# Layer 2's begin: six 1x1 products go ahead of the 3x3 taps, and three of the first sample's twelve shifted quarters are copied by VectorE

## The chip, the cores and the metric

The kernel runs on one core of a Trainium2 chip. The metric is the device time of one execution in microseconds (us), and the figure compared is the median of several runs. The profile is one further execution; all times inside it count from the first instruction.

Of the core's engines, TensorE multiplies matrices (PE in the profile, PEld for its weight loads), VectorE (DVE) and ScalarE (ACT) work element by element, GpSimd (POOL) does so too and issues DMAs through software, and SyncE (SP) issues DMAs.

## The reference

Four layers run over an activation of 8 samples, 128 channels and 56 x 56 pixels. Every layer is `x = x + conv(group_norm(x))` with 32 groups. Layer 0 is an attention over windows, layer 1 a recurrence over the pixels, layer 3 a residual block of two 3x3 convolutions. The change lies in layer 2:

```python
m3 = (j - i) % p == 0                       # p = 4
w3m = w3 * m3[:, :, None, None]
out = conv_general_dilated(x, w3m, window_strides=(1, 1), padding=((1, 1), (1, 1)))
w1m = w1 * (~m3)
out = out + einsum('oi,bihw->bohw', w1m, x)
out = out + b.sum(axis=1)[None, :, None, None]
```

So a 3x3 convolution joins only channels whose numbers are equal modulo 4, which makes four separate groups of 32 channels, and a 1x1 product joins the channels of different groups.

## The kernel before

All eight samples stay in SBUF in one tile, `X`. Layer 2 goes through them sample by sample, and through each sample in 7 blocks of 8 image rows (448 pixels). A block is numbered `n` = 7 x sample + block, 56 in all.

**The taps (`within`, line 1343).** `g3` holds, for each of the four groups (`r`), three copies of that group's 32 normalized channels, shifted by k = 0, 1 and 2 columns and stacked on 96 partitions. Twelve of these shifted quarters fill `g3` for one sample. A tap is then one product of 96 x 32 weights for one row offset `dy` and one group; a block has 3 x 4 of them. In the profile every fp32 product is two instructions, so a block's taps are 24.

**The 1x1 product (`between`, line 1351).** One product of 128 x 128 weights reads the block's rows from the normalized, zero-bordered sample (`pads`) and adds to the same PSUM bank. `add` (line 1358) then adds bank and bias to `X`. The banks come from a pool of four.

**Getting a sample ready.** `Norm` makes the group norm: `stats` (line 1281, VectorE, one instruction a block and an aggregate), a small product that averages over the groups (`mean_mm`, line 1287), four small VectorE steps (`mean_end`), a second small product (`var_mm`, line 1299), the square root on ScalarE (`root`, line 1303), the reciprocal (line 1307) and `normal` (line 1314), which writes the normalized rows to `pads`. `normal` goes by five chunks of rows, cut at 0, 10, 18, 34, 50 and 58 of the 58 padded rows. `spread` (lines 1331 and 1333) fills `g3` for one chunk: the three quarters with r equal to k are ScalarE copies, the nine others are DMAs, for every sample six from GpSimd's queue and three from SyncE's.

**What sets the order.** TensorE, ScalarE, VectorE and GpSimd take their instructions in the order in which the program lists them (`manual_schedule`); SyncE's order comes from a planner. Before the loop over blocks the program lists sample 0's norm, 26 warm-up products on TensorE (line 897), the first statistics of sample 1, sample 0's square root, five times `normal` and `spread`, the masking of the 1x1 weights (`w1` times `m1`, line 1562), the bias sum (line 1563) and sample 1's other statistics. `w1`, `m1`, the bias matrix and the batch-norm parameters are loaded by SyncE just before (lines 1251 to 1262), once memory of layer 1 is free. In the loop, `mean_mm` of the next sample follows the taps of a sample's block 1 and `var_mm` those of block 2; 1x1 products and additions come in pairs, after every odd `n`; after block 3 the next sample is normalized, and its `spread` is listed at blocks 3, 4 and 6. `g3` is single, so a chunk of it is overwritten only when the taps that read it are done.

Of the kernel before, what the change touches and what calls it, by code (L numbers as in the profile page):

```python
# [20 lines left out]
P = 128  # L21
# [25 lines left out]
def conv_stack_kernel(ctx: ExitStack, tc: tile.TileContext, a: dict, out: bass.AP):  # L47
# [1158 lines left out]
    def convolutions(held=None):  # L1206

        with ExitStack() as l2:
# [32 lines left out]


            p2 = ExitStack()
            pool2 = p2.enter_context(tc.tile_pool(name="pool2", bufs=1))
            ps_c = p2.enter_context(tc.tile_pool(name="ps_c", bufs=4, space=PSUM))
            pads = [pad3, padded(pool2, "pad2", [P, PW, PW])]
# [73 lines left out]
            def spread(b, c):  # L1320
# [4 lines left out]
                for r in range(4):  # L1325
                    for k in range(3):
                        n = hi - lo - k
                        dst = g3[k * CL : (k + 1) * CL, r, lo : lo + n]
                        src = flat[r * CL : (r + 1) * CL, lo + k : lo + k + n]
                        if r == k:  # L1330
                            nc.scalar.copy(dst, src)
                        else:
                            (nc.sync, nc.gpsimd)[(r + k) % 2].dma_start(dst, src)

            pcs = {}

            def within(n):

                i = n % NBLK
                pcs[n] = ps_c.tile([P, WS, HW], F32, name=f"pc2_{n}", tag="pc")  # L1340
                for dy in range(3):
                    for r in range(4):
                        nc.tensor.matmul(  # L1343
                            pcs[n][r * CL : (r + 1) * CL], w3[:, dy, r, :],
                            rows3[:, r, i * WS + dy : i * WS + dy + WS, :HW], start=(dy == 0), stop=False,
                        )

            def between(n):

                b, i = divmod(n, NBLK)  # L1350
                nc.tensor.matmul(  # L1351
                    pcs[n], w1, pads[b % 2][:, 1 + i * WS : 1 + (i + 1) * WS, 1 : 1 + HW], start=False, stop=True
                )
# [193 lines left out]
            with ExitStack() as order:  # L1547
# [8 lines left out]
                warm(26, ps_g, "pg")  # L1556
                norms[1].stats(0)
                norms[0].root()
                for c in range(5):
                    norms[0].normal([c])  # L1560
                    spread(0, c)
                nc.vector.tensor_mul(w1, w1, m1)
                nc.vector.tensor_reduce(bsum, bmat, AX.X, ALU.add)
                for i in range(1, NBLK):
                    norms[1].stats(i)
                for n in range(B * NBLK):
# [11 lines left out]
                    if n % 2:  # L1578
                        between(n - 1)
                        between(n)  # L1580
                        add(n - 1)
# [450 lines left out]
```

## Time and profile before

| what | us |
|---|---|
| median of 3 runs (3253.56 to 3254.7) | 3254.4 |
| the profiled execution | 3253.89 |
| its span, first to last instruction | 3251.9 |
| layer 2's first tap, after the span's start | 2653.48 |
| TensorE busy in the span | 3178.3 |

The granted TensorE clock is 0.994 of full speed over the span. The profile page gives busy shares, groups of instructions by line and the chain of waits; the trace behind it gives the same for any stretch, and a timeline. A timeline's line has the start, the duration, the engine, the line of the kernel, what is written from what, and how many instructions were merged. A bracket at its end names how long the engine was idle before and whom it waited for. `g` stands for `g3`, `pad` for `pads`, `pc` for the banks, `st_l` and `mv_l` for the statistics, `pm_l` for the mean.

### The profile page before, as it was taken

How to read it: one execution, taken by the hardware profiler on the slowest of the kernel's cores; microseconds unless marked ns; L12 is line 12 of the kernel's file. 1: busy time of each engine (PE TensorE's matmuls, PEld its weight loads, DVE VectorE, ACT ScalarE, POOL GpSimd, SP SyncE). 2: the span in 40 equal slices, each digit the busy share in tenths (PEclk: the TensorE clock that was granted, in tenths of full speed). 3: DMA queues.
4: the chain of work that ended last, by engine and by line, in shares of the span. 5: the costliest groups of instructions: out<-in, count | busy, mean ns of one | idle time of the engine just before them, and what ended most of it. 6: DMA issues, size and time to landing. Idle time of an engine off the chain costs nothing.

```text
span 3251.9 us, 104559 instructions
## 1 busy us (share of the span) xinstructions
PE 3178.3 (98%) x40784; PEld 2679.8 (82%) x40784; DVE 2270.8 (70%) x5756; ACT 1270.3 (39%) x2425; POOL 1475.3 (45%) x4147
## 2 busy tenths in 40 slices
PE   8999999999999989999999999999999999999998
PEld 5767677676766679999999999999999973399998
DVE  5888888888887866666555555555532347799998
ACT  4555555555555532221111111111111244556564
POOL 4888888888777843333222222222200036522221
PEclk8999999999999999999999999999999999999999
DMA  5555555555455421110000000000022236500001
GB/s 156 135 143 131 143 137 138 142 135 143 120 137 145 121 63 49 49 49 29 1 1 1 1 1 1 1 1 1 8 58 61 59 104 166 144 16 36 31 36 46
DMA packets 188167, 239.09 MB, mean 74 GB/s; under 512 B 42848, under 2 KB 137568, under 8 KB 187664
## 3 DMA queue, kind: packets, MB, share of 16 engines
q0 software_dynamic: 40896, 123.47, 14.0%
q1 hardware_dynamic: 130256, 101.95, 10.9%
q10 hardware_dynamic: 16512, 6.90, 0.9%
q8 instruction: 324, 5.31, 0.7%
q14 instruction: 179, 1.47, 0.2%
HBM read 133.64 MB, written 67.56 MB: 62 GB/s over the span
## 4 chain that ended last, share of the span: by engine, by line
PE 83%; DVE 10%; issue 2%; POOL 2%; ACT 1%; DMA 1%; ACTq 0%; POOLq 0%; DVEq 0%; SPq 0%
PE ps L1086 27%; PE q L1051 9%; PE po L1116 5%; PE s L539 5%; PE po L605 5%; PE pc L1343 4%; PE t L581 4%; PE plep L420 4%; PE pc3a L1663 3%; PE pc3b L1663 3%; PE pi L1021 3%; DVE nmax L546 2%; PE t L571 2%; PE pc L1351 1%; PE py L446 1%
## 5 line engine op out<-in xcount | busy, mean ns | idle before, releaser
L1086 PE MATMUL ps<-hs,w_gates 128*128 128x136 f32 x7680 | 928.8, 279 | 0.0
L1086 PEld LDWEIGHTS ps<-hs,w_gates 128*128 128x128 f32 x7680 | 911.6, 190 | 4.5
L1100 ACT ACTIVATE hs<-v 128x272 f32<-128x272 f32 x538 | 212.3, 404 | 1167.3 <-DVE v L1098 1167.3
L546 DVE TENSOR_REDUCE nmax<-s 128x2 f32<-128x512 f32 x784 | 486.3, 684 | 169.3 <-PE s L539 167.6
L591 ACT ACTIVATE e<-t 128x512 f32<-128x512 f32 x784 | 429.5, 596 | 339.8 <-PE t L581 261.8
L1098 DVE TENSOR_TENSOR v<-ps,g 128x272 f32<-128x272 f32 x538 | 216.3, 411 | 494.6 <-PE ps L1086 407.3
L1039 POOL TENSOR_TENSOR d<-inp 128x136 f32<-128x136 f32 x186 | 87.8, 472 | 789.1 <-DVE inp L1027 789.1
L498 POOL COPY ks<-kT 128x64 f32 x1568 | 297.2, 235 | 120.6 <-PE t L581 69.0
L605 PE MATMUL po<-e,ring 128*32 128x64 f32 x12544 | 244.9, 230 | 6.1 <-DVE nmax L546 5.5
L605 PEld LDWEIGHTS po<-e,ring 128*32 128x32 f32 x12544 | 217.9, 149 | 31.0 <-DVE nmax L546 7.9
L581 PE MATMUL t<-qm,ks 32*128 32x128 f32 x6272 | 237.3, 273 | 1.3 <-issue 1.3
L539 PE MATMUL s<-ks,qm 32*128 32x256 f32 x3136 | 233.9, 403 | 4.4 <-ACT vp L342 2.3
L581 PEld LDWEIGHTS t<-qm,ks 32*128 32x128 f32 x6272 | 220.1, 187 | 3.3 <-issue 2.2
L1663 PE MATMUL pc3a<-va,u_w1c_t 128*128 128x196 f32 x1152 | 198.3, 330 | 7.6 <-POOL va L1517 5.8
L1116 PE MATMUL po<-hs,xw 128*128 128x272 f32 x744 | 204.1, 397 | 0.2
L1663 PEld LDWEIGHTS pc3a<-va,u_w1c_t 128*128 128x128 f32 x1152 | 190.4, 189 | 13.6 <-POOL va L1517 11.0
L1663 PE MATMUL pc3b<-vb,u_w2c_t 128*128 128x196 f32 x1152 | 195.8, 328 | 0.0
L1663 PEld LDWEIGHTS pc3b<-vb,u_w2c_t 128*128 128x128 f32 x1152 | 191.7, 189 | 0.0
L539 PEld LDWEIGHTS s<-ks,qm 32*128 32x128 f32 x3136 | 146.6, 185 | 34.4 <-issue 4.7
L1051 PE MATMUL q<-d,mixed 128*128 128x136 f32 x1116 | 160.2, 279 | 0.5 <-DVE g L1065 0.3
L500 POOL TENSOR_TENSOR qm<-q,hmask 128x128 f32<-128x128 f32 x392 | 154.0, 393 | 0.0
L1116 PEld LDWEIGHTS po<-hs,xw 128*128 128x128 f32 x744 | 132.0, 190 | 22.1 <-ACT hs L1100 0.6
(317 smaller groups left out, 5372.3 us busy)
## 6 DMA issues: line engine op xcount, KB each, us to landing
ring<-vpix SPq DMA_DIRECT2D x1176, 32.0 KB
v<-vimg POOLq DMA_DIRECT2D x56, 290.0 KB, 4.0
v<-vimg POOLq DMA_DIRECT2D x56, 289.5 KB, 4.8
v<-vimg POOLq DMA_DIRECT2D x56, 289.0 KB, 5.7
kept<-g SPq DMA_DIRECT2D x56, 272.0 KB, 2.4
g<-kept SPq DMA_DIRECT2D x56, 272.0 KB, 2.6
xkeep<-X POOLq DMA_DIRECT2D x56, 224.0 KB, 2.7
vimg<-vrow POOLq DMA_DIRECT2D x54, 232.0 KB, 2.7
```

Source lines behind the costliest of these rows:

```text
L498: nc.gpsimd.tensor_copy(kw[:, t : t + 1, :], ks[b][:, bass.ds(at, 1), :])
L539: nc.tensor.matmul(s_["s"][g][:, o, :], w["qm"][h].rearrange("p h x -> p (h x)"), w["kw"][h], start=True, stop=True,)
L546: nc.vector.tensor_reduce(s_["nmax"][:, :, g], s_["s"][g], AX.X, ALU.max, negate=True)
L581: nc.tensor.matmul(s_["t"][g][:, o, c], w["kw"][h, c * P : (c + 1) * P], w["qm"][h].rearrange("p h x -> p (h x)"), start=False, stop=(o == ...
L591: nc.scalar.activation(s_["e"][g], s_["t"][g], AF.Exp)
L605: mm = nc.tensor.matmul(po[g * CL : (g + 1) * CL, h, o], flat[:, at : at + 8 * CL - 7 : 8], s_["e"][g][:, o, c, h * WPX : (h + 1) * WPX], ...
L1051: nc.tensor.matmul(q[n // 3][:, n % 3], w, x, start=True, stop=True)
L1086: nc.tensor.matmul(ps[f][:, i], whh[:, k, m * P : (m + 1) * P], prev[k // 2][:, (s - 1) % 2, k % 2].rearrange("p c b -> p (c b)"), start=( ...
L1098: nc.vector.tensor_tensor(v[:, i : i + n], ps[f][:, i : i + n], x, ALU.add)
L1100: nc.scalar.activation(to, x, AF.Tanh)
L1116: nc.tensor.matmul(po, wout[:, k, :], hs[k // 2][:, :, k % 2], start=(k == 0), stop=(k == KH - 1))
L1663: nc.tensor.matmul(bank[:, half].rearrange("p (y x) -> p y x", x=H4), u[:, dy, k, :], v[:, k, i * RB + dy : i * RB + dy + RB, :], start=(d ...
```

## The change

- The pool of banks has six instead of four.
- The 1x1 products of the first six blocks are issued before the loop, behind the normalization of sample 0, and open their banks; the taps of these blocks then add to the bank and close it. Later blocks are as before.
- For sample 0 alone, the three quarters of group r = 3 are VectorE copies. Of the six DMAs left per chunk, three are on SyncE's queue and three on GpSimd's (before: three and six).
- The masking of `w1` stands ahead of sample 0's square root and reciprocal, not behind the normalization.
- `spread` of a chunk is listed one `normal` later, and the first statistics of sample 1 join the six others behind all this.

```diff
+            AHEAD = 6
-            ps_c = p2.enter_context(tc.tile_pool(name="ps_c", bufs=4, space=PSUM))
+            ps_c = p2.enter_context(tc.tile_pool(name="ps_c", bufs=AHEAD, space=PSUM))
...
                         if r == k:
                             nc.scalar.copy(dst, src)
+                        elif b == 0 and r == 3:
+                            nc.vector.tensor_copy(dst, src)
                         else:
-                            (nc.sync, nc.gpsimd)[(r + k) % 2].dma_start(dst, src)
+                            even = (r - k) % 3 == 2 if b == 0 else (r + k) % 2 == 0
+                            (nc.sync if even else nc.gpsimd).dma_start(dst, src)
...
             def within(n):
                 i = n % NBLK
-                pcs[n] = ps_c.tile([P, WS, HW], F32, name=f"pc2_{n}", tag="pc")
+                if n >= AHEAD:
+                    pcs[n] = ps_c.tile([P, WS, HW], F32, name=f"pc2_{n}", tag="pc")
                 for dy in range(3):
                     for r in range(4):
                         nc.tensor.matmul(
                             pcs[n][r * CL : (r + 1) * CL], w3[:, dy, r, :],
-                            rows3[:, r, i * WS + dy : i * WS + dy + WS, :HW], start=(dy == 0), stop=False,
+                            rows3[:, r, i * WS + dy : i * WS + dy + WS, :HW],
+                            start=(dy == 0 and n >= AHEAD), stop=(dy == 2 and n < AHEAD),
+                            skip_group_check=True,
                         )
             def between(n):
                 b, i = divmod(n, NBLK)
+                if n < AHEAD:
+                    pcs[n] = ps_c.tile([P, WS, HW], F32, name=f"pc2_{n}", tag="pc")
                 nc.tensor.matmul(
-                    pcs[n], w1, pads[b % 2][:, 1 + i * WS : 1 + (i + 1) * WS, 1 : 1 + HW], start=False, stop=True
+                    pcs[n], w1, pads[b % 2][:, 1 + i * WS : 1 + (i + 1) * WS, 1 : 1 + HW],
+                    start=(n < AHEAD), stop=(n >= AHEAD), skip_group_check=True,
                 )
...
                 warm(26, ps_g, "pg")
-                norms[1].stats(0)
+                nc.vector.tensor_mul(w1, w1, m1)
                 norms[0].root()
-                for c in range(5):
-                    norms[0].normal([c])
-                    spread(0, c)
-                nc.vector.tensor_mul(w1, w1, m1)
+                for c in range(6):
+                    if c < 5:
+                        norms[0].normal([c])
+                    if c > 0:
+                        spread(0, c - 1)
+                for n in range(AHEAD):
+                    between(n)
                 nc.vector.tensor_reduce(bsum, bmat, AX.X, ALU.add)
-                for i in range(1, NBLK):
+                for i in range(NBLK):
                     norms[1].stats(i)
...
                     if n % 2:
-                        between(n - 1)
-                        between(n)
+                        if n >= AHEAD:
+                            between(n - 1)
+                            between(n)
                         add(n - 1)
                         add(n)
```

## The prediction

> **What bounds the kernel now.** I read the profile page's busy shares first, then the windows of layer 2, its chain of waits, the timeline of its first 20 us, and last the groups kept apart by shape, for prices.
>
> ```profile
> span 3251.9 us, 104559 instructions
> ...
> PE 3178.3 (98%) x40784; PEld 2679.8 (82%) x40784; DVE 2270.8 (70%) x5756; ACT 1270.3 (39%) x2425; POOL 1475.3 (45%) x4147
> ```
>
> TensorE is busy in 98% of the span, so a change in order can only win where it is idle. The windows of layer 2's first two samples (columns: stretch, its length, then busy time and count of each engine, clock, DMA share, GB/s):
>
> ```profile
> 2653.40:2675.60 22.20, 22.09 (x172) 9.69 (x176) 10.57 (x19) 9.62 (x15) 13.06 (x28) 1.00 0.74 195
> 2675.60:2698.00 22.40, 22.40 (x190) 7.96 (x186) 12.69 (x26) 13.14 (x18) 16.44 (x34) 1.00 0.73 195
> ```
>
> From its first tap to the layer's end TensorE does not pause, and VectorE (third pair) has about half of its time free. The chain of waits over the begin (start, us, what):
>
> ```profile
> 2650.96 2.52 DMA g<-pad
> 2653.48 5.17 PE pc L1343 x48
> 2658.64 0.31 PE pm_l L1287 x2
> 2658.95 1.62 PE pc L1351 x4
> ...
> 2666.61 1.71 PE pc L1351 x4
> 2668.32 4.65 PE pc L1343 x48
> ```
>
> Two blocks' taps take 4.65 us undisturbed, 5.17 at the start; two blocks' 1x1 products take 1.71. The timeline around it:
>
> ```profile
> 2644.75 7.68 PE L897 MATMUL warm<-c_gavg 128*128 128x128 f32 x52
> ...
> 2645.42 3.12 DVE L1314 TENSOR_SCALAR pad<-X,gm_l,r_l 128x504 f32<-128x504 f32 x5
> ...
> 2645.98 0.43 SPq L1255 DMA_DIRECT2D m<-in_m_dram  x1
> ...
> 2648.46 0.28 DVE L1562 TENSOR_TENSOR w<-w,m 128x128 f32<-128x128 f32 x1
> ...
> 2648.85 3.25 DVE L1281 BATCH_NORM_STATS2 st_l<-X 128x6 f32<-128x448 f32 x6
> ...
> 2653.48 5.17 PE L1343 MATMUL pc<-g,w 96*32 96x448 f32 x48 [1.05 <-DMA g<-pad]
> ...
> 2658.99 0.16 DVE L1291 COPY gm_l<-pm_l 128x1 f32<-128x1 f32 x1 [6.03 <-PE pm_l L1287]
> ```
>
> Two things are to be seen. The warm-up products end at 2652.43, so only 1.05 us of idle TensorE lies ahead of the taps. And VectorE has sample 1's statistics ready six microseconds before TensorE asks for their mean (L1287, after the second block): that slack is what the change spends.
>
> **Ceiling of the gain.** The TensorE work is the same before and after. What idleness can go is 1.05 us ahead of the taps, 5.17 - 4.65 = 0.52 in the first two blocks, and 0.03 in the third: 1.60 us.
>
> **Products ahead.** Six products are 3 x 1.71 = 5.13 us. They follow the warm-up: 2652.43 to 2657.56, then two blocks of taps (4.65) to 2662.21. Their inputs are there: the last of them starts at 2656.7, and the fourth piece of the normalization it reads ends near 2655 by the sum below. The flags and the two more banks cost nothing: before, TensorE never waits for VectorE to free a bank in this layer, so a deeper ring hides nothing more; were a bank late, block 6 would wait for the addition of block 0, which ends some 9 us ahead of it.
>
> **The mask product moved up on VectorE.** It now stands ahead of the reciprocal and waits for m1, which SP issues at 2645.98. The old wait instruction for it, at 2648.1, lasted 0.05 us, so the data was there; the shortest landing of any spread transfer is 1.8, so not before 2647.8. I take 2648.1, the row of that very transfer. Queued behind it: reciprocal, five normalizations, fifteen copies, seven statistics; waiting on those: ScalarE's copies, both DMA queues, TensorE. Start to start, product to next 0.19 and reciprocal to normalization 0.20: the first normalization starts at 2648.49 instead of 2645.42, 3.07 later. SP loses nothing, since parameter loads hold its queue until 2649.38; POOL's first issue goes from 2646.51 to about 2649.6.
>
> **Three quarters by VectorE.** Fifteen copies, 10,077 elements in all (three times 3,364 columns, less the shifts). Rows:
>
> ```profile
> L1314 DVE TENSOR_SCALAR pad<-X,gm_l,r_l 128x504 f32<-128x504 f32 x1 | 0.8, 799 | 0.0
> ...
> L1176 DVE COPY first<-hs 128x256 f32<-128x256 f32 x2 | 0.6, 288 | 0.3 <-ACT hs L1100 0.3
> ...
> L1386 DVE TENSOR_SCALAR u_w1c_t<-u_w1c_t 128x768 f32<-128x768 f32 x1 | 0.5, 547 | 0.0
> ...
> L1375 DVE COPY u_w1c_t<-t_w1c_t 128x384 f32<-128x384 f32 x1 | 0.4, 406 | 0.0
> ```
>
> 256 and 768 elements at 288 and 547 ns give 0.51 ns an element and 0.16 us fixed. The 504 row (nine rows, an unbroken run into a padded one) is much slower, while the even 896 of the same line takes 738. Five of the fifteen have odd length (k = 1), so they might be slow as the 504 is; but the 384 copy is of three rows, odd too and alike on both sides as our copies are, and is fast. I take the fast price: 15 x 0.15 + 10.08 x 0.52 = 7.5, and 0.03 more each, the step between dependent VectorE instructions in the timeline: 7.95 us. The other end, every copy at one element per 1.04 ns (what the plain 128x136 copy out of PSUM, 295 ns, leaves after the fixed part): 12.75 + 0.45 = 13.2. The low end is 6.5, should they overlap by some 0.07 as the normalizations do (0.74 us long, 0.66 apart).
>
> **VectorE's sum.** 2648.49, five normalizations 3.04 (2645.42 to 2648.46), copies 7.95, the bias sum 0.20, seven statistics and their aggregate 3.28 + 0.53 + 0.34 = 4.15 (the first of them was free while the variance was awaited; now it is in line): 2663.83, and 0.10 to reach TensorE. TensorE wanted the mean at 2662.21: **a new stall of 1.72 us**. Sums of the ends: 2662.4 or less with the low price (no stall worth naming), 2669.2 with the high one (7.0).
>
> **Six quarters by DMA.** POOL issues 15 instead of 30 and SP 15 as before. At 0.50 each POOL is done near 2658 instead of 2664.65. Chunk 1, needed at 2659.9 by block 1, is issued by SP at 2653.2 at the latest, as before, and the landing seen on SP there is 5.3: 2658.5. ScalarE's fifteen copies (11.6) end at 2661, each chunk ahead of its block. Both are hidden by the 5.13 us of products that now go first; a transfer later by more than 1.4 us would show one for one, first by eating the stall at L1287 and then beyond it.
>
> **A rule against it.** POOL's first two issues, beside the normalizations, read 0.88 and 0.65 us instead of 0.50:
>
> ```profile
> 2646.51 0.88 POOL L1333 DMA_DIRECT2D g<-pad  x1 [0.73 <-DVE pad L1314]
> 2647.39 0.65 POOL L1333 DMA_DIRECT2D g<-pad  x1
> 2648.04 0.50 POOL L1333 DMA_DIRECT2D g<-pad  x1
> ```
>
> At 0.88 for all fifteen, chunk 1's last is issued by 2654.9 and lands 3.6 later at 2658.5: still hidden. The Trainium skill, "SBUF — State Buffer", section "Who interferes with whom", has a VectorE copy in its two-port mode shut GpSimd out of the shared port for the whole instruction; the page's example is a GpSimd DMA going from about 620 to 3100 ns. An estimate by that factor of five is 2.5 us an issue, chunk 2 then landing near 2675 where 2664 is needed, some 11 us lost. The rows go against a factor that large.
>
> **The next sample's begin.** What is late next: block 7, sample 1's first. Its normalization starts when block 3 is added, and its first chunk's last POOL issue stands at 2673.59 and lands 2.7 later: 2676.29, that is 7.97 us after block 3 ends (2668.32). Before, block 7 starts 8.68 us after it; without the products of blocks 4 and 5 it could start after 6.98, so it now waits for the DMA at 7.97. The change gets back 0.71 here and not 1.71.
>
> **Sum.** Mean product ends 2663.93 + 0.31, two blocks 2 x 2.39 and the variance 0.31: block 3 ends at 2669.33. Block 7 starts at 2669.33 + 7.97 = 2677.30 against 2677.00 before (2674.67 + 2.33): **+0.3 us**. From there the order is the old one and TensorE has no slack to give it back. The profiled execution took 3253.89 (span 3251.9); the median, 3254.4, is 0.5 above. With it: 3254.7.
>
> **The rivals.**
> 1. The cover holds fully: copies overlap, m1 is early, the DMA for block 7 too. All 1.60 us are won: 3252.8. For it: the low ends above; against it: VectorE must save 1.7 us.
> 2. The copies run at the slow price: 5.25 us more in the same stall, +5.5: 3259.9. For it: the 504 row; against it: the three copies and scalings above.
> 3. Slower: VectorE's copies wait at the port for POOL's issues, one each, 15 x 0.50 = 7.5 us more ahead of L1287: +7.8, 3262.2. It decides from 6.2 us, or 0.41 a copy. For it: the two stretched issues show that the engines meet; against it: the normalizations beside them kept their time (742 ns for 896 elements, 738 over all nine).
>
> A measurement of this kernel can tell about 0.2%, 6.5 us, from no change: 3247.9 to 3260.9.
>
> **How the numbers follow.** Forecast (between rival 1 and +3 us) 0.62, rival 1 0.12, rival 2 0.13, rival 3 0.11; 0.02 for a gain past the ceiling. Same is 0.62 + 0.12 + 0.13 = 0.87, slower 0.11, faster 0.02. The range takes in the forecast and rivals 1 and 2: 3252.6 to 3260.5.
>
> **What would show it.** After: six products right behind the warm-up, taps near 2657.6; the first normalization near 2648.5; copies of 0.39 to 0.63 us; a wait of TensorE for L1287's statistics of 1 to 2 us; block 7 waiting on a transfer by about 1 us. Wrong if m1 is loaded in another place of SP's order, if copies take over 0.8 us, if POOL's issues pass 1.5 us, or if TensorE stalls in a later sample.

## The result and the profile after

The changed kernel takes 3261.68 us (median of 19 runs, 3257.26 to 3265.68) where the kernel before takes 3255.74 (19 runs, 3253.0 to 3260.56). The ratio is 1.0017, with a 95% interval of 1.0011 to 1.0023: 5.9 us more. That is less than the 0.2% that the prediction took as the least that can be told from no change, but the interval separates it from zero, and it lies 1.2 us above the range that was forecast (3252.6 to 3260.5). The prediction was wrong: it had +0.3 us. Two executions of all those below, one of e10_half_filled and the profiled one of b_again, took 5334 and 4541 us at a granted clock of 0.56 and 0.65, and no comparison uses them.

The page of the changed kernel, first the span and then the busy time of each engine:

```profile
span 3260.6 us, 104551 instructions
...
PE 3184.0 (98%) x40784; PEld 2680.5 (82%) x40784; DVE 2280.4 (70%) x5771; ACT 1271.0 (39%) x2425; POOL 1474.0 (45%) x4132
```

TensorE has as many instructions as before and is busy 5.7 us longer (3184.0 against 3178.3). So a part of the loss is no idleness at all: the same products took longer. VectorE has 15 instructions more and GpSimd 15 fewer, which are the copies and the DMAs they replace.

The timeline around layer 2's begin (start, duration, engine, line, what is written from what, count, in brackets the idle time before):

```profile
2645.24 6.05 PE L897 MATMUL warm<-c_gavg 128*128 128x128 f32 x52
2646.49 0.43 SPq L1256 DMA_DIRECT2D m<-in_m_dram  x1
2648.66 0.29 DVE L1567 TENSOR_TENSOR w<-w,m 128x128 f32<-128x128 f32 x1 [3.77 <-DMA m<-in_m_dram]
2649.06 1.22 DVE L1315 TENSOR_SCALAR pad<-X,gm_l,r_l 128x504 f32<-128x504 f32 x2
2650.31 1.39 DVE L1334 COPY g<-pad 32x580 f32<-32x580 f32 x3
2651.13 3.19 PE L1360 MATMUL pc<-pad,w 128*128 128x448 f32 x8
2654.55 1.93 DVE L1334 COPY g<-pad 32x928 f32<-32x928 f32 x3
2654.58 1.78 PE L1360 MATMUL pc<-pad,w 128*128 128x448 f32 x4 [0.26 <-DVE pad L1315]
2656.28 4.72 PE L1348 MATMUL pc<-g,w 96*32 96x448 f32 x48
2657.22 3.16 DVE L1334 COPY g<-pad 32x928 f32<-32x928 f32 x6
2660.59 3.77 DVE L1282 BATCH_NORM_STATS2 st_l<-X 128x6 f32<-128x448 f32 x7
2664.40 0.34 DVE L1284 BATCH_NORM_AGGREGATE mv_l<-st_l 128x2 f32<-128x42 f32 x1
2664.80 0.59 PE L1288 MATMUL pm_l<-mv_l,c_gavg 128*128 128x1 f32 x2 [3.80 <-DVE mv_l L1284]
2665.32 4.71 PE L1348 MATMUL pc<-g,w 96*32 96x448 f32 x24
2670.47 12.85 PE L1348 MATMUL pc<-g,w 96*32 96x448 f32 x102
```

The mask waits 3.77 us for its load, and everything on VectorE stands behind it: normalization, copies, statistics. TensorE, done with the first two blocks at 2661.0, waits 3.80 us for sample 1's statistics. What the forecast has nothing of comes after that: block 2's 24 taps take 4.71 us, and the next 102 take 12.85, where runs of the same taps below take 2.46 and 10.6. The windows over the same stretch (stretch, length, then busy time and count of PE, PEld, DVE, ACT and POOL, then the granted clock, DMA share and GB/s) say why:

```profile
2656.00:2661.00 5.00, 5.00 (x49) 1.45 (x48) 4.87 (x10) 4.88 (x6) 2.86 (x5) 1.00 0.93 238
2661.00:2665.00 4.00, 0.20 (x2) 0.20 (x2) 3.96 (x9) 0.59 (x2) 0.00 (x0) 0.98 0.76 228
2665.00:2670.00 5.00, 5.00 (x27) 1.34 (x27) 3.12 (x9) 0.00 (x0) 0.00 (x0) 0.50 0.02 6
2670.00:2673.00 3.00, 3.00 (x22) 1.24 (x22) 0.68 (x1) 0.26 (x1) 0.00 (x0) 0.50 0.00 0
2673.00:2680.00 7.00, 7.00 (x68) 2.10 (x64) 4.72 (x7) 2.52 (x4) 1.65 (x4) 0.85 0.15 38
```

The granted clock is 0.50 from 2665 to 2673 and averages 0.85 to 2680: half speed for about 10 us, some 5 us of work lost, right behind a wait of 3.8 us. In the kernel before, the clock dips on the warm-up products, whose result nobody waits for (0.57 over 2644.7 to 2648.5), and stays at 1.00 from the first tap on.

The Trainium skill, "TensorE: Matmul & The Clock Gate", sections "What's actually happening" and "Why this matters for your kernels", states that an idle window of about 3.4 us halves the clock, that this window runs on its own and is not started by the kernel, and asks for no gaps above some 3 us. The 3.80 us here agree. The runs below agree with a window that runs on its own (the clock changes only in steps of 3.41 us, as shown under e0_third), but not with 3 us as a safe bound: the clock fell behind waits of 2.74 and of 1.55 us as well, and did not behind one of 2.70.

**A sum by stages.** Layer 1, whose code is the same, ends up to 5.6 us earlier or later from profile to profile, so stages are counted from the first small product of sample 0's mean (2642.69 on the trace before, 2643.17 after). Before, layer 2 lasts 201.94 us from there (201.22 in a second profile of the same kernel); after, 210.25: 8.3 more.

- Up to sample 1's mean product: 21.63 after, 15.88 before, but with six 1x1 products done, which last 5.13 by the forecast's row. Lost: 0.62.
- From there to the pair of products of blocks 6 and 7: 21.15 after; 20.68 before with those 5.13 in it, so 15.55. Lost: 5.60, almost all of it the clock.
- From there to layer 3: 167.47 after, 165.38 before. Lost: 2.1, in samples whose code did not change.

### The profile page after: what moved, and what is told of

Its sections match the earlier page's. It is cut to its first block, busy times and chain, and to the rows that moved or that the text cites. A ratio compares the mean times of both kernels' runs of the same rounds, so it can differ in the third digit from the quotient of the medians.

```text
span 3260.6 us, 104551 instructions
## 1 busy us (share of the span) xinstructions
PE 3184.0 (98%) x40784; PEld 2680.5 (82%) x40784; DVE 2280.4 (70%) x5771; ACT 1271.0 (39%) x2425; POOL 1474.0 (45%) x4132
## 4 chain that ended last, share of the span: by engine, by line
PE 84%; DVE 10%; issue 2%; POOL 2%; ACT 1%; DMA 1%; ACTq 0%; POOLq 0%; SPq 0%; DVEq 0%
PE ps L1086 27%; PE q L1051 9%; PE po L605 5%; PE s L539 5%; PE po L1116 5%; PE pc L1348 4%; PE t L581 4%; PE plep L420 4%; PE pc3a L1677 3%; PE pc3b L1677 3%; PE pi L1021 3%; DVE nmax L546 2%; PE t L571 2%; PE py L446 1%; PE pc L1360 1%
```

## The experiments

The theory taken to the chip: VectorE's line, with the wait of the mask, the 15 copies and the statistics all ahead of the aggregate, decides when sample 1's mean is ready, whatever TensorE does; TensorE's wait for it costs its length and then half the clock. Rivals: the products ahead cost something themselves, by taking the cover from sample 1's transfers or by their banks; the mask's wait is hidden; the six transfers left per chunk, or the copies beside GpSimd, are what is late; the loss lies in later samples.

Every kernel here computes the full result. In the table, times are medians, with the ratio to runs of the kernel before that were measured beside them; the stages come from each run's profile in us from the zero point above: first tap, sample 1's aggregate ready, TensorE's wait for the mean, clock behind it, products of blocks 6 and 7, layer 3.

| kernel | time | ratio [95%] | tap | ready | wait | clock behind | 6, 7 | layer 3 |
|---|---|---|---|---|---|---|---|---|
| before | 3255.74 | 1 | 10.79 | 9.78 | 0 | full | 36.56 | 201.94 |
| before, b_third | 3253.86, one run | | 10.73 | 9.79 | 0 | full | 36.40 | 201.22 |
| changed | 3261.68 | 1.0017 [1.0011, 1.0023] | 13.11 | 21.57 | 3.80 | half for 10.2 us | 42.78 | 210.25 |
| changed, e0_again | 3262.45 | 1.0022 [1.0013, 1.0031] | 14.21 | 21.62 | 2.74 | half for 6.8 us | 41.25 | 208.64 |
| changed, e0_third | 3260.14, one run | | 14.22 | 21.58 | 2.70 | full | 37.96 | 204.83 |
| e1_filled_wait | 3261.43 | 1.0020 [1.0011, 1.0029] | 15.70 | 21.64 | 0, filled | full | 39.72 | 208.03 |
| e2_mask_later | 3255.41 | 1.0003 [0.9994, 1.0012] | 12.59 | 18.76 | 1.51 | full | 35.21 | 202.16 |
| e3_products_only | 3253.60 | 0.9995 [0.9986, 1.0004] | 14.21 | 9.79 | 0 | full | 34.78 | 200.76 |
| e4_copies_only | 3262.23 | 1.0015 [1.0006, 1.0024] | 9.82 | 18.24 | 1.55 | half for 3.4 us | 39.66 | 206.70 |
| e5_products_less_warm | 3255.07 | 0.9996 [0.9987, 1.0005] | 11.32 | 9.80 | 0 | full | 34.36 | 198.40 |
| e6_change_less_warm | 3263.50 | 1.0017 [1.0008, 1.0027] | 13.26 | 21.73 | 3.81 | half for 10.2 us | 43.09 | 210.36 |
| e7_mask_early_only | 3259.38 | 1.0010 [1.0001, 1.0019] | 9.87 | 12.83 | 0 | full | 39.33 | 204.85 |
| e8_all_mended | 3255.12 | 0.9998 [0.9989, 1.0007] | 11.31 | 14.63 | 0 | full | 33.03 | 199.17 |
| e9_stats_first | 3257.62 | 1.0004 [0.9995, 1.0013] | 14.22 | 17.66 | 0 | full | 36.05 | 202.29 |
| e10_half_filled | 3263.03 | 1.0018 [1.0009, 1.0028] | 14.22 | 21.70 | 1.15 | full | 38.18 | 205.41 |
| e10_second | 3262.77, one run | | 14.14 | 21.75 | 1.28 | full | 38.24 | 207.73 |
| e11_more_warm | 3260.55 | 1.0025 [1.0014, 1.0035] | 18.33 | 21.50 | 0 | full | 39.21 | 207.82 |

**e0_again: the changed kernel once more.** No edit.

> The changed kernel once more. Theory A (a stall and a clock drop): VectorE's sum alone sets when the mean of sample 1 is ready, so the wait of TensorE at that product is again 3.5 to 4.1 us, the granted clock in the 10 us behind it is again near 0.5, and the time is 5 to 7 us above the kernel before. Rival B (the clock dips anyway, and where it falls is luck): in this execution the dip lies on the warm-up products, as in the profile of before, the taps run at full clock, and the time is 1 to 3 us above the kernel before.

The aggregate is ready at 21.62 as in the first profile. TensorE's wait is shorter, 2.74 us, because its 26 warm-up products took 7.68 us this time and not 6.05: the same products, the clock dipping on them in one profile and not in the other. The clock fell behind this wait too (0.67, then 0.50, then 0.77 in the windows to 2676), so block 2 took 3.81 us. Theory A holds, though the wait is 1 us shorter than it had.

**e1_filled_wait: TensorE is kept busy in the wait.**

```diff
                     within(n)
+                    if n == 1:
+                        warm(14, ps_g, "pg")
```

> Fourteen warm-up products (about 3.3 us) are put into the stall, ahead of the mean of sample 1; nothing else is changed. Theory A: the wait is as long as before but busy, the clock stays at 1.00, blocks 2 and 3 take 2.4 us each instead of 4.7, and the time is 4 to 6 us below the changed kernel, at most 2 us above the kernel before. Rival B (dips anyway): no difference to the changed kernel beyond 1 us. Rival C (the copies or the transfers cost the time, not the clock): the time stays 5 to 6 us above the kernel before.

The timeline of TensorE in this kernel, behind the first two blocks:

```profile
2657.35 4.72 PE L1348 MATMUL pc<-g,w 96*32 96x448 f32 x48
2662.00 3.39 PE L897 MATMUL warm<-c_gavg 128*128 128x128 f32 x28
2665.23 0.28 PE L1288 MATMUL pm_l<-mv_l,c_gavg 128*128 128x1 f32 x2
2665.44 2.46 PE L1348 MATMUL pc<-g,w 96*32 96x448 f32 x24
2668.14 10.61 PE L1348 MATMUL pc<-g,w 96*32 96x448 f32 x102
```

With no idle wait the clock stays at 1.00, and the next taps take 2.46 and 10.61 us instead of 4.71 and 12.85. So it is the idle wait that the clock follows. The timed median is hardly better for it (3261.43, where 4 to 6 us less than the changed kernel were expected): the filler overshoots by 1.9 us (mean at 23.58), and from blocks 6 and 7 to layer 3 this kernel takes 168.3 us instead of 165.4.

**e2_mask_later: only the mask goes back, behind the second normalization.**

```diff
                 warm(26, ps_g, "pg")
-                nc.vector.tensor_mul(w1, w1, m1)
                 norms[0].root()
...
                         spread(0, c - 1)
+                    if c == 1:
+                        nc.vector.tensor_mul(w1, w1, m1)
```

> The masking product goes behind the first chunk's copies, so the normalization no longer waits for the mask. Theory A: VectorE's line ends 2.9 us earlier, the wait of TensorE shrinks from 3.8 to about 0.9 us, the clock stays at 1.00, and the time is 6 to 9 us below the changed kernel, that is 0 to 2 us below the kernel before. Rival C: the wait for the mask is hidden by the warm-up products, and the time falls by less than 2 us against the changed kernel.

VectorE no longer waits for the load, and the aggregate is ready at 18.76 instead of 21.6, 2.8 earlier. TensorE waits 1.51 us:

```profile
2660.76 0.34 DVE L1284 BATCH_NORM_AGGREGATE mv_l<-st_l 128x2 f32<-128x42 f32 x1
```

```profile
2654.93 4.72 PE L1348 MATMUL pc<-g,w 96*32 96x448 f32 x48
2661.16 0.38 PE L1288 MATMUL pm_l<-mv_l,c_gavg 128*128 128x1 f32 x2 [1.51 <-DVE mv_l L1284]
2661.47 2.59 PE L1348 MATMUL pc<-g,w 96*32 96x448 f32 x24
```

The clock does not fall, and 3255.41 us is not told apart from before. With the mask's 2.8 us gone the loss is gone too, though all the copies are still there.

**e3_products_only: the products ahead and the six banks, without copies, new split of the queues, or moves on VectorE.**

```diff
-                        elif b == 0 and r == 3:
-                            nc.vector.tensor_copy(dst, src)
...
-                            even = (r - k) % 3 == 2 if b == 0 else (r + k) % 2 == 0
+                            even = (r + k) % 2 == 0
...
-                nc.vector.tensor_mul(w1, w1, m1)
+                norms[1].stats(0)
                 norms[0].root()
-                for c in range(6):
-                    if c < 5:
-                        norms[0].normal([c])
-                    if c > 0:
-                        spread(0, c - 1)
+                for c in range(5):
+                    norms[0].normal([c])
+                    spread(0, c)
+                nc.vector.tensor_mul(w1, w1, m1)
```

> Only the six products ahead and the six banks; VectorE copies nothing, DMA moves nine quarters as before, mask and statistics stand where they stood. Theory A: no wait at the mean, full clock, and all that can be won is the idleness ahead of the taps less what block 7 gives up: 0 to 2 us below the kernel before. Rival D (the products ahead do the harm, by uncovering the next sample's transfers or by holding back the taps): 2 us or more above the kernel before.

The aggregate is ready at 9.79 as in before, nothing waits, and layer 2 takes 200.76 us, 0.5 to 1.2 less than before. The products ahead do no harm by themselves and win about what idleness there was; the time, 3253.60, is not told apart from that of before.

**e4_copies_only: the kernel before with the copies, the split of the queues, and `spread` one `normal` later.**

```diff
+                        elif b == 0 and r == 3:
+                            nc.vector.tensor_copy(dst, src)
                         else:
-                            (nc.sync, nc.gpsimd)[(r + k) % 2].dma_start(dst, src)
+                            even = (r - k) % 3 == 2 if b == 0 else (r + k) % 2 == 0
+                            (nc.sync if even else nc.gpsimd).dma_start(dst, src)
...
-                for c in range(5):
-                    norms[0].normal([c])
-                    spread(0, c)
+                for c in range(6):
+                    if c < 5:
+                        norms[0].normal([c])
+                    if c > 0:
+                        spread(0, c - 1)
```

> Only the quarters: VectorE copies three, DMA moves six, spread is listed one normalization later; the 1x1 products, the mask, the four banks and the first statistics stand as in the kernel before. Theory A (VectorE's line sets the mean of sample 1): the mean is ready about 4 us after block 1 of before would have asked less 2 (by VectorE's prices some 17 us after the first small product, where block 1 ends 14.5 to 15.5 after it), so TensorE waits 1.5 to 2.5 us, with or without a clock drop, and the time is 1 to 5 us above the kernel before. Rival E (the copies are harmless and fewer transfers help): no wait at the mean, the taps start 0.5 to 1 us sooner, and the time is 0 to 1.5 us below the kernel before.

Without the products ahead there is nothing to cover 8.5 us more on VectorE: the aggregate comes at 18.24, where before TensorE asks at 15.88. The wait and what follows it, in TensorE's timeline:

```profile
2665.55 0.38 PE L1287 MATMUL pm_l<-mv_l,c_gavg 128*128 128x1 f32 x2 [1.55 <-DVE mv_l L1283]
2665.79 2.89 PE L1354 MATMUL pc<-pad,w 128*128 128x448 f32 x4
2668.61 2.96 PE L1346 MATMUL pc<-g,w 96*32 96x448 f32 x24
2671.81 2.46 PE L1346 MATMUL pc<-g,w 96*32 96x448 f32 x24
```

A wait of 1.55 us was enough here: the clock is 0.62 and then 0.82 for some 6 us, products of 1.76 us take 2.89 and taps of 2.46 take 2.96. Behind e2's 1.51 it was not. The length of the wait does not decide alone; what does is seen under e0_third.

**e7_mask_early_only: the kernel before with only the mask moved ahead of the root.**

```diff
+                nc.vector.tensor_mul(w1, w1, m1)
                 norms[0].root()
...
-                nc.vector.tensor_mul(w1, w1, m1)
                 nc.vector.tensor_reduce(bsum, bmat, AX.X, ALU.add)
```

> The kernel before with one instruction moved: the masking product ahead of the reciprocal. Theory A: the normalization waits for the load of m1 and starts 3 us later, POOL's six transfers of chunk 0 with it, so the taps start 2.5 to 3.5 us later and the time is 2 to 4 us above the kernel before, more by up to 3 if the longer idle stretch halves the clock of the first taps. Rival H (the warm-up products and SP's later transfers hide it): less than 1 us above the kernel before.

```profile
2649.59 0.29 DVE L1558 TENSOR_TENSOR w<-w,m 128x128 f32<-128x128 f32 x1 [3.33 <-DMA m<-in_m_dram]
```

```profile
PE pc L1343 <- DMA g<-pad: 1.7, 3, 0.7
```

The mask waits for its load (VectorE's timeline), the normalization and all transfers start later, and TensorE's waits now hold three for `g3`, 1.7 us in all, inside the first two blocks. From first tap to sample 1's mean product it takes 9.73 us where the kernel before takes 5.10. The median is 1.0010 of before (1.0001 to 1.0019), layer 2 is 2.9 to 3.6 us longer. The move is not hidden even with VectorE's six microseconds of slack, because it delays the normalization and not only the statistics.

**e9_stats_first: the change with its early mask, but sample 1's statistics ahead of the last two chunks' copies.**

```diff
                 warm(26, ps_g, "pg")
+                norms[1].stats(0)
                 nc.vector.tensor_mul(w1, w1, m1)
...
-                for c in range(6):
-                    if c < 5:
-                        norms[0].normal([c])
-                    if c > 0:
+                for c in range(5):
+                    norms[0].normal([c])
+                    if 0 < c < 4:
                         spread(0, c - 1)
...
-                nc.vector.tensor_reduce(bsum, bmat, AX.X, ALU.add)
-                for i in range(NBLK):
+                for i in range(1, NBLK):
                     norms[1].stats(i)
+                spread(0, 3)
+                spread(0, 4)
+                nc.vector.tensor_reduce(bsum, bmat, AX.X, ALU.add)
```

> The changed kernel with one thing altered: the statistics of sample 1 stand ahead of VectorE's copies of chunks 3 and 4 (the first of them in its old gap). The mask is as early as in the change. Theory A: the mean is ready some 17.7 us after the first small product instead of 21.6, block 1 ends 17.8 to 19.3 after it, so the wait of 2.7 to 3.8 us and the half clock behind it are gone though every instruction is still there: 5 to 7 us below the changed kernel, within 2 us of the kernel before. Rival C (the copies as such, or the mask's wait, cost the time): 2 to 4 us below the changed kernel at most.

VectorE does the same work in another order. The aggregate is ready at 17.66, TensorE asks at 18.86 and does not wait:

```profile
2660.72 4.72 PE L1348 MATMUL pc<-g,w 96*32 96x448 f32 x48
2665.36 0.38 PE L1288 MATMUL pm_l<-mv_l,c_gavg 128*128 128x1 f32 x2
2665.68 2.46 PE L1348 MATMUL pc<-g,w 96*32 96x448 f32 x24
```

With mask and copies kept, 3257.62 us is no longer told apart from before. e2 leaves the copies and takes the mask's wait out of the line, e9 leaves the mask's wait and takes two chunks' copies and one statistics instruction out of it; either is enough. So the wait for the aggregate, with what it brings, is most of the loss, and it comes from the sum of the two ahead of the statistics.

**e6_change_less_warm and e11_more_warm: the change with 13 and with 38 warm-up products instead of 26.**

```diff
-                warm(26, ps_g, "pg")
+                warm(13, ps_g, "pg")
```

```diff
-                warm(26, ps_g, "pg")
+                warm(38, ps_g, "pg")
```

> The changed kernel with 13 warm-up products in place of 26. Theory A: VectorE's line does not move, so the mean is ready 21.6 us after the first small product as in the two profiles of the changed kernel; what TensorE does sooner it waits longer for: the taps start up to 2 us sooner, the wait grows to 4 to 6 us, the clock falls, and the time is within 2 us of the changed kernel, 4 to 8 us above the kernel before. Rival G (the start of the taps counts, the mean does not): the time falls by as much as the taps start sooner, 2 to 4 us below the changed kernel.

> The changed kernel with 38 warm-up products instead of 26, so that TensorE starts the six products and the taps about 2.8 us later and arrives at the mean when VectorE has it (21.6 us after the first small product). Theory A with the clock as a cause of its own: the taps start 15.9 to 18.5 us after the first small product, the wait at the mean is under 1.2 us, blocks 2 and 3 run at full clock, and although everything starts later the time is 2 to 5 us below the changed kernel. Theory A2 (the wait alone costs, the clock's dip falls somewhere in any case): blocks 2 and 3 start when they did, and the time is within 1.5 us of the changed kernel.

The warm-up takes 4.78 us with 13 products and 11.61 with 38, and the first tap comes at 13.26 and at 18.33. The aggregate is ready at 21.73 and 21.50. TensorE's beginning moves by 5 us and the aggregate by 0.2: it hangs on VectorE alone. With 13 products TensorE waits 3.81 us and loses its clock; with 38 it neither waits nor loses it. Yet e11's time, 3260.55, is no better than the change's: its mean is 1.34 us later than in e0_third, and from blocks 6 and 7 to layer 3 it takes 168.6 us.

**e10_half_filled and e10_second: seven filling products where e1 has fourteen.**

```diff
                     within(n)
+                    if n == 1:
+                        warm(7, ps_g, "pg")
```

> The changed kernel with seven warm-up products (1.6 us) in the wait, instead of fourteen, which outlasted it. Theory A: the mean comes at its old time (21.6 us after the first small product), the rest of the wait is under 2.2 us, the clock stays at 1.00 through blocks 2 and 3 (2.4 us each), and the time is 2 to 4 us below the changed kernel, 2 to 4 above the kernel before. Rival B (dips anyway): as the changed kernel.

> The changed kernel with seven products in the wait, a second profile. Theory A: the times of this kernel fall into two heaps, 3258.6 to 3259.5 and 3262.8 to 3267.1; the first profile was of the lower heap and at full clock, so one of the upper heap shows half clock in blocks 2 and 3. Theory A2: an execution of the upper heap is at full clock there too, and loses its time elsewhere.

Both profiles show waits of 1.15 and 1.28 us, no overshoot to speak of, and a full clock. Layer 2 takes 205.41 and 207.73 us. The timed runs lie between 3258.6 and 3267.1 with a median of 3263.03: the gain that the profiles show is not in the time. The second profile is of the upper heap of times (3262.77) and at full clock, so theory A2 holds for it: it loses 2.3 us more than the first from blocks 6 and 7 to layer 3 (169.49 against 167.23).

**e0_third and b_third: a further profile of the changed kernel and of the kernel before.** No edit.

> The changed kernel, a third profile, for the spread of the warm-up (6.1 and 7.7 us so far), of the wait (3.8 and 2.7) and of the half clock behind it. Theory A: the mean at 21.6 us after the first small product once more, a wait of 1.3 to 3.9 us by how long the warm-up took, and half clock behind it if the wait is over 2.5 us.

> The kernel before, a second usable profile: the later samples (products of blocks 6 and 7 to layer 3's first product) took 165.4 us in the first. Theory A: 164 to 168, as in the other runs, so that differences of 2 us there between single profiles tell nothing. Rival D: 165.4 within 0.3.

The changed kernel with a wait of 2.70 us and a full clock behind it:

```profile
2660.18 4.72 PE L1348 MATMUL pc<-g,w 96*32 96x448 f32 x48
2667.60 0.38 PE L1288 MATMUL pm_l<-mv_l,c_gavg 128*128 128x1 f32 x2 [2.70 <-DVE mv_l L1284]
2667.91 2.49 PE L1348 MATMUL pc<-g,w 96*32 96x448 f32 x24
2670.65 13.35 PE L1348 MATMUL pc<-g,w 96*32 96x448 f32 x120
```

Without the half clock, layer 2 takes 204.83 us, 2.9 more than the first profile of before; with it, 208.64 and 210.25. The difference of the medians, 5.9 us, lies between.

A half clock behind every wait over 2.5 us was expected, and this one has none. What decides is where the wait falls. In every trace the granted clock changes only at points that lie whole multiples of 3.41 us apart. Cut at these points, the two profiles with nearly the same wait read as follows (stretch, length, TensorE busy and count, granted clock, DMA share, GB/s), first e0_again:

```profile
2660.73:2664.14 3.41, 2.74 (x32) 1.00 0.84 208
2664.14:2667.55 3.41, 1.34 (x14) 1.00 0.53 180
2667.55:2670.97 3.42, 3.42 (x22) 0.50 0.00 0
2670.97:2674.38 3.41, 3.41 (x20) 0.50 0.00 0
2674.38:2677.79 3.41, 3.41 (x40) 1.00 0.02 5
```

and e0_third:

```profile
2663.00:2666.41 3.41, 1.90 (x23) 1.00 0.97 234
2666.41:2669.83 3.42, 2.23 (x24) 1.00 0.27 101
2669.83:2673.24 3.41, 3.41 (x38) 1.00 0.00 0
```

In e0_again 2.07 us of idleness fall into one piece, and the next two pieces run at half speed. In e0_third a cut divides the wait into 1.51 and 1.19 us, and the clock stays. In layer 2 of the 17 profiles in the table, counted from the first small product, all 17 pieces at full clock with 1.59 us of idleness or more were followed by half clock, and none with 1.52 or less was; of four in between, two were. Why half speed then lasts one, two or three pieces, with TensorE busy throughout, is open.

The kernel before takes 164.82 us from blocks 6 and 7 to layer 3, 0.56 less than in its first profile: single profiles differ there without any change.

**b_again: the kernel before, timed once more.** No edit.

> The kernel before once more, for a second profile: whether its later samples (products of blocks 6 and 7 to the end of layer 2, 165.4 us in the first profile) and its warm-up (7.7 us) vary from execution to execution. Theory A: 165.4 to 167 us and no wait at the mean; the 0.6 to 2.9 us by which the later samples of all other runs lie above 165.4 are then partly the chance of that one execution. Rival D (the change uncovers transfers of later samples): 165.4 within 0.3 us again.

3256.4 us, 1.0001 of the other runs of the same kernel (0.9992 to 1.001): what is called a loss above is not the scatter of two builds. It has no profile to answer its question; b_third has.

**e5_products_less_warm and e8_all_mended: is there a version that beats both?** e5 is e3 with half of the warm-up, as an edit of e3:

```diff
-                warm(26, ps_g, "pg")
+                warm(13, ps_g, "pg")
```

> The products alone, as in the run without copies, with 13 warm-up products in place of 26. Theory A: the warm-up products hold the six products back until 7 us after the variance; with half of them the products run while the transfers of chunk 0 are under way, the taps start when they did in the kernel before (some 10.8 us after the first small product, or up to 1 us later) with six products done, and the time is 3 to 5 us below the kernel before. Rival F (the shorter warm-up lets the clock fall to half, so the products and the first taps run at half speed): the time is within 1.5 us of the kernel before, or above it.

e8 is the change with half of the warm-up, the mask behind the second normalization, and the statistics as in e9, as an edit of the change:

```diff
-                warm(26, ps_g, "pg")
+                warm(13, ps_g, "pg")
-                nc.vector.tensor_mul(w1, w1, m1)
+                norms[1].stats(0)
                 norms[0].root()
-                for c in range(6):
-                    if c < 5:
-                        norms[0].normal([c])
-                    if c > 0:
+                for c in range(5):
+                    norms[0].normal([c])
+                    if 0 < c < 4:
                         spread(0, c - 1)
+                    if c == 1:
+                        nc.vector.tensor_mul(w1, w1, m1)
...
-                nc.vector.tensor_reduce(bsum, bmat, AX.X, ALU.add)
-                for i in range(NBLK):
+                for i in range(1, NBLK):
                     norms[1].stats(i)
+                spread(0, 3)
+                spread(0, 4)
+                nc.vector.tensor_reduce(bsum, bmat, AX.X, ALU.add)
```

> The changed kernel with four edits: the mask behind the first two normalizations, the first statistics of sample 1 back in their gap and the other six ahead of the copies of chunks 3 and 4, 13 warm-up products for 26. Theory A: by VectorE's measured prices the mean is ready 15.0 us after the first small product and block 1 ends some 15.4 after it, so there is no wait and no clock drop; the taps start 10.8 to 11.5 us after it with six products done, and the time is 3 to 5 us below the kernel before. Rival E2 (VectorE's copies cost something beside their place in line, by holding POOL's transfers or the additions): less than 2 us below the kernel before, or above it.

Their layer 2 is the shortest of all, 198.40 and 199.17 us, 2.1 to 3.5 less than before in its two profiles. The times are 0.9996 (0.9987 to 1.0005) and 0.9998 (0.9989 to 1.0007) of before: no version here beats it by more than can be measured, where 3 to 5 us were expected. Both profiled executions are the fastest of their kernel's runs (3252.01 and 3253.11), so the stages show these kernels at their best. What copies, mask and split were added for is not needed: e5 has none of them.

## Why the prediction was wrong

**Right.**

- The mask waits for `m1`: the first normalization, 2649.06, is 2648.58 on the time scale of the trace before (layer 2 starts 0.48 later in the trace after), forecast 2648.49.
- The copies take the fast price: 0.39 to 0.64 us each and 1.39 + 1.26 + 1.93 + 3.16 = 7.74 in all, forecast 7.95. Rival 2 falls.
- Rival 3 falls with the same number: the copies have no room for waits at the port. GpSimd's issues beside them, 12 in 6.93 us, are 0.58 each instead of 0.50. The factor of five in the example of the Trainium skill, "SBUF — State Buffer", section "A bandwidth-pool intuition that's wrong (but worth ruling out)" (about 620 to 3100 ns for a GpSimd DMA beside a VectorE copy), is not seen here.
- VectorE's sum: the mean product was to start at 21.24 us after the zero point; it started at 21.63, 21.67 and 21.64 in three profiles, 0.4 late.
- Block 7 waits for its transfers: forecast 0.99 us; in e0_third blocks 3 to 7 take 13.27 us (2670.65 to 2683.92) where five blocks take 5 x 2.39 = 11.95, 1.3 more. TensorE's weight loads wait there 0.9 us for a DMA and 0.7 for ScalarE's copies.

**Rival 1, the full cover,** falls with the wait. **The size of the stall** was missed: forecast 1.72, measured 3.80, 2.74, 2.70. VectorE's 0.4 is the smaller part. The rest is TensorE coming sooner: it was to ask at 19.52 and did at 17.83 (21.63 - 3.80), 18.93 and 18.94. The step behind it is "They follow the warm-up: 2652.43 to 2657.56": it took 7.68 us as fixed, and the same 26 products took 6.05 once; and three pairs at 1.71 each were 5.13, where six products in a row take 4.63 (2655.55 to 2660.18 in e0_third). By itself this costs nothing, since what TensorE gains ahead of the stall it waits in it, and only 0.62 us were lost up to the mean against 21.24 - 15.88 - 5.13 = 0.23 in the forecast's sum. But it stretched the idle time.

**The clock** is the step that failed: the sum has no term for what a stall does to the work behind it. "Mean product ends 2663.93 + 0.31, two blocks 2 x 2.39" reckons with 2.39 us a block, and block 2 alone took 4.71, 3.81 and 2.49. From the mean to blocks 6 and 7 the three profiles lost 5.60, 4.03 and 0.77 us. The last has a full clock; so the clock's price is 4.8 and 3.3 us where it fell. The trace of before showed that a wait can do this: its warm-up products ran at 0.57 behind a wait of 1.5 us, and the forecast took their 7.68 us as they stood.

**"From there the order is the old one"** failed too. From blocks 6 and 7 to layer 3 the changed kernel takes 167.5, 167.4 and 166.9 us, before 165.4 and 164.8. Part lies at blocks 8 and 9, sample 1's second pair: 8.51, 8.91 and 8.19 us from pair to pair, before 7.55 and 8.01. What brings it is not shown: e3 and e5, with products ahead but no copies, have 8.17 and 8.28, e4, with copies but no products ahead, has 8.45, and the two profiles of before differ by 0.46 themselves. In these two profiles the second pair of samples 1, 3, 5 and 7 takes 7.36 to 8.78 us, where other pairs give an estimate of 7.03 without waiting (6.35, and 0.25 and 0.43 more for the two small products). So TensorE does wait in the later samples, where the prediction read that it "does not pause". The rest is at the begins of samples 2 and 6, where a pair takes 7.05 to 7.18 and 7.44 to 7.67 us in the three profiles; in both profiles of before, in e3, e5 and e7 it takes 6.60 each time. There GpSimd pauses for 2.9 us in the midst of its issues, for nothing that the trace shows. GpSimd's timeline after:

```profile
2699.39 1.51 POOL L1337 DMA_DIRECT2D g<-pad  x3 [4.41 <-issue]
2703.82 7.50 POOL L1337 DMA_DIRECT2D g<-pad  x15 [2.91 <-issue]
...
2799.47 8.51 POOL L1337 DMA_DIRECT2D g<-pad  x17 [2.96 <-issue]
```

and before, at the same count of issues, where the trace names the taps as what ended the pause:

```profile
2683.05 5.01 POOL L1333 DMA_DIRECT2D g<-pad  x10 [2.95 <-PE pc L1343]
...
2777.02 3.99 POOL L1333 DMA_DIRECT2D g<-pad  x8 [2.99 <-PE pc L1343]
```

Counted through layer 2, a pause of 2.87 to 3.08 us stands ahead of GpSimd's 49th and 170th DMA issue in all 17 profiles. With 30 DMAs for sample 0 (before, e3, e5, e7) these two belong to the fourth chunk of samples 1 and 5; with 15 fewer, to the first chunk of samples 2 and 6, which the sample's first taps read. At sample 6 the pair of products takes 7.31 to 9.34 us in all twelve profiles with 15 fewer; at sample 2 it takes more than 6.60 in six of them (the change three times, e2, e4, e9). So the pause keeps its place in GpSimd's order of issues, and the change moves the work that meets it. What causes it is open: a packet of a queue that loads instructions lies in the second pause in 12 of the 17 profiles, in the first in none.

**What adds up.** At full clock: 0.62 + 0.77 + 1.5 = 2.9 us; with the clock's 3.3 to 4.8 and the scatter of the later samples, 6.7 to 8.3. The medians differ by 5.9. The share of the clock in runs without a profile can be estimated, since the record lists the granted clock of each run to three decimals. The 11 runs of e0_again average 0.99273 and the 33 of the kernel before measured beside them 0.99415: (0.99415 - 0.99273) x 3258 = 4.6 us of full speed (1.8 either way at 95%), where the mean times differ by 7.1. The 19 runs of the result average 0.99316, all 111 runs of the kernel before that were measured beside the experiments 0.99406: 2.9 us (1.1 either way) of 5.6. What is left, 2.5 and 2.7 us, is near the 2.9 at full clock. By this estimate the clock brings half of the loss or somewhat more.

One thing does not fit. e1, e10 and e11, whose profiles show a full clock behind the wait, are not faster than the change in the time. In e1 the clock is back in the timed runs too (0.99400, a loss of 0.5 us, 2.0 either way), so e1 loses its time elsewhere: its mean comes 1.9 us later, and it takes 168.3 us from blocks 6 and 7 to layer 3. e11's mean comes 1.3 us later, with 168.6 us there; e10 takes 167.2 and 169.5 there in its two profiles. That accounts for a part, and the rest is open.

## What to carry to other kernels

An instruction that is moved up an in-order queue takes its wait along, and that wait then stands ahead of all that follows. Slack on an engine that is not the bottleneck is to be counted over its whole line up to the thing the bottleneck waits for: 3 us of waiting and 8 us of copies together passed it here, and taking the wait (e2) or two chunks' copies (e9) out of that line was enough to bring the time back. And a new stall of the matrix engine is to be priced with a possible half clock behind it, 1.7 to 5 us of lost work here for waits from 1.55 us on, not by its length.

## What the runs showed of the hardware that was not expected

- The same 26 warm-up products took 6.05, 7.40, 7.56, 7.68 or 8.95 us, depending on where the half clock fell.
- The clock halved behind waits for the mean of 1.55, 2.74, 3.80 and 3.81 us and not behind 1.15, 1.28, 1.51 and 2.70. It changes only at points whole multiples of 3.41 us apart, and half speed lasted 3.4, 6.8 or 10.2 us. It followed when 1.59 us or more of idleness lay between two such points, and not when 1.52 or less did.
- GpSimd's DMA issues pause 2.87 to 3.08 us ahead of the 49th and the 170th in layer 2, in all 17 profiles, whatever sample these belong to.
